# An attention layer's output projection: from four-head accumulation to seven block products

## The chip, the cores and the metric

The kernel runs on one core of one Trainium2 chip. The metric is device time in microseconds (us) of one execution. The engines are named as the profile names them: PE is TensorE's matmuls and PEld its weight loads, DVE is VectorE, ACT is ScalarE, POOL is GpSimd, and SP is SyncE, whose queue issues every DMA of this kernel.

## The reference

One transformer layer on 8 sequences of 512 tokens with 512 features: latent attention with 16 heads, then a gated feed-forward part. Cut to what matters:

```python
x = x + attn(layernorm(x))          # x: (8, 512, 512), float32
x = x + ffn(layernorm(x))

def attn(h):
    q = rmsnorm(h @ wq_a.T) @ wq_b.T           # 16 heads of 128 + 64 (rotary)
    kv_c, k_pe = split(h @ wkv_a.T)            # latent of 128, rotary of 64
    k_nope, v = split(rmsnorm(kv_c) @ wkv_b.T) # 16 heads of 128 and 128
    attn = softmax(q @ k.T * SCALE)            # per batch and head, 512 x 512
    out = (attn @ v).reshape(b, s, 16 * 128)
    return out @ wo.T                          # 2048 -> 512
```

The kernel multiplies the value and output weights of each head into one 128x512 matrix ahead of time ("wvo"), so that a head contributes (attn @ latent) @ wvo to the output. The output projection is then, for each batch, a product of a 512x2048 matrix (16 heads of 128) with a 2048x512 one, added to x.

## The kernel before, in words

`attention` runs over 8 batches x 16 heads x 4 query tiles of 128 tokens: 512 steps (L549). A dictionary `later` holds, per step, the functions to be called at it, and the loop at L613 calls them in order; so the order of issue is written out by hand, though the framework's scheduler may move an instruction among others that don't depend on it, and chooses the buffers and waits.

A step issues the scores of its tile (`scores`, L487): one f32 matmul of 128x512 and two in the single-pass f32r format, into a PSUM tile `sc`, of which there are four (L253). VectorE takes the row maximum (L499), ScalarE the exponential with its sum (L502). One step later VectorE divides (L507) and transposes 32x32 blocks (L156); at every second step the result goes through DRAM and comes back in key-major order as `prT` (`send`, L161: a store and four loads on SyncE's queue). Five steps after a head's last tile `attend` (L512) multiplies by the latent and ScalarE copies the result to `o` (L520), with 128 features on the partitions and 512 tokens along the row. `project` (L452) makes the next head's queries and issues the rotary part, whose sum is made on GpSimd (L360).

After every fourth head, `output` (L526) adds a group of four heads to x: for each of four token tiles, four f32 matmuls of 512 columns accumulate over the heads into a PSUM tile of the pool `ps_mm` (two buffers, L252), and VectorE adds that to `x` (L537). The five functions go to steps 7, 8, 11, 12 and 13 after the last tile of the group's last head (L626). The last of them stores x to DRAM when the fourth group is done (L541). The four `wvo` tiles stay in SBUF for all batches; `fold_o` (L319) makes them during batch 0.

While batch b runs, `prepare` (L579) loads x of batch b+1 and `latents` (L365) makes its normalised, transposed latents, in pieces spread over heads 5 to 12; x is held in two buffers. GpSimd and VectorE also round the feed-forward weights to 8 bits in pieces (`round_piece`, L329) during batches 1 to 6. In the last batch those weights are loaded into the places of weights no longer needed (L600 to L606): the three parts of `wu` where `wvo` lay.

`ffn` (L640) then goes over the 8 batches: matmuls in f32r, two for each product (a high and a low part of the operand).

[...] In `attention` two go to `ps_mm`, four to the scores, one to transposes and one to `attend`.

Of the kernel before, what the change touches and what calls it, by code (L numbers as in the profile page):

```python
# [32 lines left out]
F32 = mybir.dt.float32  # L34
# [7 lines left out]
P = 128  # L42
# [7 lines left out]
G = 4  # L50
# [34 lines left out]
class Layer:  # L85
    def __init__(self, ctx, tc, ins, out):
# [3 lines left out]
        self.xp = ctx.enter_context(tc.tile_pool(name="x", bufs=2))  # L90
        self.dram = dram = ctx.enter_context(tc.tile_pool(name="scratch", bufs=1, space=bass.MemoryType.DRAM))
        self.ident = self.wp.tile([P, P], F32, tag="ident", name="ident")
        make_identity(nc, self.ident)
        self.eps_ln = self.wp.tile([P, 1], F32, tag="eps_ln", name="eps_ln")
# [5 lines left out]
        self.ffn_w = {}  # L100
        self.scratch = {
            (w, i // n): dram.tile([P, n, H], F32R, tag=f"{w}d{i // n}", name=f"{w}d{i // n}")
            for w, n in (("wg", 3), ("wu", 4), ("wd", 4))
            for i in range(0, NI, n)
        }
        self.size = {"wg": 3, "wu": 4, "wd": 4}
# [9 lines left out]
    def load_ffn(self, w, k, pool, tag):  # L116

        n = self.size[w]
        t = pool.tile([P, n, H], F32R, tag=tag, name=f"{w}{k}")
        self.nc.sync.dma_start(t.bitcast(F32), self.scratch[w, k].bitcast(F32))  # L120
        for j in range(n):
            self.ffn_w[w, k * n + j] = t[:, j, :]
# [64 lines left out]
    def ffn_parts(self):  # L187
        return (
            self.xp.tile([P, NC, S], F32R, tag="lat", name="yh"),
# [25 lines left out]
    def ffn_normed_blocks(self, x, small, work):  # L215
# [4 lines left out]
        y = self.wp.tile([P, 2, NQ, NC, 2 * Q], F32, tag="tok", name="y")  # L220
# [5 lines left out]
        def apply(t):  # L226
            xn = work.tile([P, H], F32, tag="xn", name="xn")
# [18 lines left out]
    def attention(self):  # L246
        tc, nc, ins, wp, xp = self.tc, self.nc, self.ins, self.wp, self.xp
        with ExitStack() as ctx:
# [4 lines left out]
            ps_sc = ctx.enter_context(tc.tile_pool(name="ps_sc", bufs=4, space=PSUM))  # L253
            ps_t = ctx.enter_context(tc.tile_pool(name="ps_t", bufs=1, space=PSUM))
            ps_av = ctx.enter_context(tc.tile_pool(name="ps_av", bufs=1, space=PSUM))

            def load_x(src):

                x = xp.tile([P, NT, H], F32, tag="x", name="x")
# [8 lines left out]
            wlr = wp.tile([P, NC, RL], F32, tag="wlr", name="wlr")  # L268
# [5 lines left out]
            xs = {0: x}  # L274
# [4 lines left out]
            wqp_s, wa_s, wvo_s = [], [], []  # L279
# [39 lines left out]
            def fold_o(h):  # L319

                g, j = divmod(h, G)
                wv, wo = fold.pop(("o", h))
                if j == 0:
                    wvo_s.append(wp.tile([P, G, H], F32, tag=f"wvo{g}", name=f"wvo{g}"))
                ps = ps_mm.tile([P, H], F32, tag="mm", name="wvo_ps")
                nc.tensor.matmul(ps, wv, wo, start=True, stop=True)  # L326
                nc.scalar.activation(wvo_s[g][:, j, :], ps, AF.Identity, scale=knw)
# [37 lines left out]
            def latents(b):  # L365


                x = xs[b]
# [400 lines left out]
```

## Time and profile before

| what | us |
|---|---|
| three timed runs | 2802.70, 2803.81, 2803.94 |
| median | 2803.81 |
| the profiled execution | 2803.76 |
| its span, from first to last instruction | 2802.0 |
| TensorE's granted clock in it | 0.997 of full |

Busy time of the engines in stretches of the span that are about a batch of attention each, and in the feed-forward part, in us:

| from | to | PE | DVE | ACT | POOL |
|---|---|---|---|---|---|
| 600 | 875 | 275.0 | 190.4 | 93.2 | 33.0 |
| 1150 | 1425 | 274.7 | 193.1 | 92.5 | 32.4 |
| 1980 | 2270 | 286.1 | 173.8 | 83.3 | 10.5 |
| 2270 | 2800 | 526.5 | 195.0 | 163.5 | 126.8 |

A row says for how long each engine had an instruction running in the stretch. Matmuls overlap their neighbours, so a share near the whole means that one was always in flight, and not that the array was at its best.

All DMAs together move 359.9 MB, at 128 GB/s over the span; their packets keep the 16 DMA engines busy for 41% of it. The largest parts are the stores and loads of the transposed weights of attention: 256 stores of 512 KB (median 2.8 us from issue to landing) and 1024 loads of 128 KB (3.5 us).

### The profile page before, as it was taken

What the parts mean: (1) busy time and instruction counts of PE and PEld (TensorE: products, weight loads), DVE (VectorE), ACT (ScalarE), POOL (GpSimd) and SP (SyncE); (2) the same over time, 40 slices, a digit from 0 to 9 for tenths busy, and PEclk for the clock granted to TensorE, in tenths of its full rate; (3) what the DMA queues carried; (4) which work ended last, traced back from release to release, by engine and by line L of the source; (5) the groups of instructions that cost most, each with busy time, mean ns of one, the idle gap of its engine ahead of it and who ended that gap; (6) DMA issues with size and microseconds to landing.
All of it is one profiled execution on the core that took longest, in us unless ns stands there. A gap on an engine that the chain in (4) does not pass through costs nothing.

```text
span 2802.0 us, 27010 instructions
## 1 busy us (share of the span) xinstructions
PE 2777.7 (99%) x8496; PEld 1566.6 (56%) x8496; DVE 1706.1 (61%) x3584; ACT 916.3 (33%) x1956; POOL 351.4 (13%) x341
## 2 busy tenths in 40 slices
PE   8999999999999999999999999999999999999999
PEld 4555445444544454455444544554444468888887
DVE  5756676776676767676766676666666634433332
ACT  3333333333332333233333332333233233222222
POOL 2000101210020011000200021000000012222222
PEclk9999999999999999999999999999999999999999
DMA  4634454445445534453445344533455541111110
GB/s 141 195 117 139 135 165 129 140 146 158 122 134 153 169 106 143 150 166 111 139 143 165 117 147 137 165 113 120 148 167 162 149 151 60 61 64 64 60 64 19
DMA packets 240047, 359.87 MB, mean 128 GB/s; under 512 B 27168, under 2 KB 190112, under 8 KB 237216
## 3 DMA queue, kind: packets, MB, share of 16 engines
q1 hardware_dynamic: 239904, 358.14, 41.3%
q8 instruction: 68, 1.11, 0.2%
q14 instruction: 75, 0.61, 0.1%
HBM read 190.27 MB, written 167.77 MB: 128 GB/s over the span
## 4 chain that ended last, share of the span: by engine, by line
PE 98%; DVE 1%; ACT 1%; DMA 0%; POOL 0%; issue 0%; SPq 0%; ACTq 0%; POOLq 0%; DVEq 0%
PE wo_ps L534 16%; PE sc L495 16%; PE av L517 15%; PE qn_ps L467 11%; PE sc L497 8%; PE pu L668 6%; PE pg L668 6%; PE pd L694 6%; PE qpe_ps L461 6%; PE lr_ps L393 4%; PE ln_pt L148 1%; PE wvo_ps L326 0%; PE lat_pt L426 0%; PE wa_ps L311 0%; DMA x<-in_hid 0%
## 5 line engine op out<-in xcount | busy, mean ns | idle before, releaser
L502 ACT ACTIVATE pr<-sc,nmax 128x512 f32<-128x512 f32 x512 | 351.6, 687 | 781.3 <-DVE nmax L499 585.2
L497 PE MATMUL sc<-kpe,qpe 128*128 128x512 f32 x1024 | 530.4, 597 | 0.3 <-DVE qpe L479 0.3
L495 PE MATMUL sc<-lat,qn 128*128 128x512 f32 x1024 | 523.3, 592 | 2.0 <-ACT qn L469 1.6
L499 DVE TENSOR_REDUCE nmax<-sc 128x1 f32<-128x512 f32 x512 | 349.5, 684 | 257.1 <-PE sc L497 254.7
L534 PE MATMUL wo_ps<-wvo,o 128*128 128x512 f32 x1024 | 466.0, 595 | 3.5 <-ACT o L520 3.2
L517 PE MATMUL av<-prT,kvt 128*128 128x512 f32 x1024 | 461.2, 592 | 0.0
L156 DVE STREAM_TRANSPOSE block<-pr 128x512 f32<-128x512 f32 x512 | 358.3, 705 | 10.3
L467 PE MATMUL qn_ps<-lat,wa 128*128 128x512 f32 x768 | 352.7, 593 | 0.0
L497 PEld LDWEIGHTS sc<-kpe,qpe 128*128 128x128 f32 x1024 | 194.0, 190 | 246.3 <-issue 235.1
L517 PEld LDWEIGHTS av<-prT,kvt 128*128 128x128 f32 x1024 | 192.3, 190 | 216.1 <-issue 207.0
L534 PEld LDWEIGHTS wo_ps<-wvo,o 128*128 128x128 f32 x1024 | 191.5, 190 | 206.0 <-issue 180.5
L495 PEld LDWEIGHTS sc<-lat,qn 128*128 128x128 f32 x1024 | 191.0, 190 | 162.9 <-issue 139.9
L507 DVE TENSOR_SCALAR pr<-pr,rden 128x512 f32<-128x512 f32 x512 | 273.0, 533 | 13.5
L467 PEld LDWEIGHTS qn_ps<-lat,wa 128*128 128x128 f32 x768 | 145.8, 190 | 161.5 <-issue 150.1
L360 POOL TENSOR_TENSOR roped<-rope_own,rope_sw 128x512 f32<-128x512 f32 x72 | 94.4, 1312 | 1072.7 <-DVE rope_sw L359 899.2
L678 DVE SCALAR_TENSOR_TENSOR fuse<-pu,us,gate 128x512 f32<-128x512 f32 x96 | 71.8, 749 | 203.3 <-PE pu L668 192.2
L682 POOL TENSOR_TENSOR fl<-fuse,fh 128x512 fp32r<-128x512 f32 x96 | 126.8, 1322 | 454.5 <-ACT fh L681 374.7
L506 DVE RECIPROCAL rden<-den 128x1 f32<-128x1 f32 x512 | 77.9, 152 | 164.3 <-ACT pr L502 162.4
L461 PE MATMUL qpe_ps<-lat,wqp 128*128 128x512 f32 x384 | 177.5, 596 | 0.0
L74 POOL TENSOR_TENSOR q_r<-raw,q_m 128x256 f32<-128x256 f32 x72 | 54.0, 750 | 872.9 <-DVE q_m L72 760.6
L668 PE MATMUL pg<-yh,wg 128*128 128x512 f32 x384 | 151.8, 395 | 1.0 <-DVE x L537 0.8
L668 PE MATMUL pu<-yh,wu 128*128 128x512 f32 x384 | 152.4, 397 | 0.0
(93 smaller groups left out, 2884.7 us busy)
## 6 DMA issues: line engine op xcount, KB each, us to landing
way<-block SPq DMA_DIRECT2D x256, 512.0 KB, 2.8
prT<-way SPq DMA_DIRECT2D x1024, 128.0 KB, 3.5
x<-in_hid SPq DMA_DIRECT2D x32, 256.0 KB, 4.6
x<-x SPq DMA_DIRECT2D x8, 1024.0 KB, 4.4
out<-o SPq DMA_DIRECT2D x32, 256.0 KB, 2.0
fx<-x SPq DMA_DIRECT2D x7, 1024.0 KB, 5.1
way<-y_block SPq DMA_DIRECT2D x14, 512.0 KB, 2.6
y<-way SPq DMA_DIRECT2D x56, 128.0 KB, 2.8
```

The lines of the kernel that those rows point to most:

```text
L156: self.nc.vector.transpose(out[:, :, :, i : i + Q].rearrange("p c k i -> p k c i"), x.rearrange("p (k c j) -> p k c j", c=NQ, j=Q),)
L461: nc.tensor.matmul(ps, wqp_s[g][:, r, pj * P : (pj + 1) * P], lat[:, r, :], start=r == 0, stop=r == NR - 1)
L467: nc.tensor.matmul(ps, wa_s[g][:, j, r, :], lat[:, r, :], start=r == 0, stop=r == NR - 1)
L495: nc.tensor.matmul(sc, qn[:, q], lat[:, NR, :], start=True, stop=False)
L497: nc.tensor.matmul(sc, qpe[:, h % 2, q], kpe[:, part, :], start=False, stop=part == 1)
L499: nc.vector.tensor_reduce(nmax, sc, AX.X, ALU.max, negate=True)
L502: nc.scalar.activation(pr, sc, AF.Exp, bias=nmax, accum_out=den)
L507: nc.vector.tensor_scalar(pr, pr, rden, None, ALU.mult)
L517: nc.tensor.matmul(av, kvt[:, kt, :], prT[:, :, :, kt, :], start=kt == 0, stop=kt == NT - 1)
L534: nc.tensor.matmul(ps, o[j][:, t * P : (t + 1) * P], wvo_s[g][:, j, :], start=j == 0, stop=j == G - 1)
L668: nc.tensor.matmul(ps, w[name, i][:, c * P : (c + 1) * P], y[k][:, c, :], start=c == 0 and k == 0, stop=c == NC - 1 and k == 1,)
L694: nc.tensor.matmul(pd, f[:, i, t * P : (t + 1) * P], w["wd", i], start=i == 0 and f is fh, stop=i == NI - 1 and f is fl,)
```

## The change

Strassen's scheme, in Winograd's form with seven products, replaces the eight block products of a 2x2 block multiplication. A group of four heads is two head pairs. For each pair the left matrix has two token halves (256 tokens each) as block rows and the even and odd head as block columns; the right one (`wvo`) has the even and odd head as block rows and two feature halves of 256 as block columns.

- `sums` makes the four sums of the left blocks of a pair, on GpSimd, one step after the pair's second `attend`: S3 = A11 - A21, S1 = A21 + A22 (in the place of A21), S2 = S1 - A11, S4 = A12 - S2.
- `fold_o` writes the three blocks that are used as they are into a tile of seven (`wst`), and GpSimd makes the four sums T1 to T4 in batch 0. The tile is stored to DRAM (`wst_d`), since seven blocks of all groups don't fit in SBUF beside the rest. From batch 1 on, `load_wst` loads each group's tile in four pieces, into two buffers that rotate.
- `output` makes seven products. Each is four matmuls with 256 columns (two token tiles of the half x two head pairs, accumulated). They share PSUM tiles: `u` (a bank of its own, pool `ps_o`) takes A11 B11, then on top of it S2 T2, S3 T3 and A22 T4; `v` takes S1 T1 and then S4 B22; `z` takes A12 B21. After each product VectorE adds the tile as it then stands to a quarter of x, seven additions of 128x512 elements in all. In four of the five functions there are two, one, two and two products.
- The bank for `u` comes from the scores, which have three tiles instead of four.
- x has one buffer in place of two: `prepare` loads x of the next batch into the tile `tok`, in which `latents` also writes its result, and x is loaded once more, at step 3 of head 3 of its own batch, to be added to.
- `wu` is kept in two parts of six instead of three of four; the first is loaded into a `wst` buffer in the last head of attention, the second after attention, and `wd` is loaded whole at the start of the feed-forward part. There, tiles take other places (`y`, `xn`, `o`, and x in turn in two tiles).

```diff
-        self.xp = ctx.enter_context(tc.tile_pool(name="x", bufs=2))
+        self.xp = ctx.enter_context(tc.tile_pool(name="x", bufs=1))
...
+        self.size = {"wg": 3, "wu": 6, "wd": 4}
...
+        self.wst_d = [
+            dram.tile([P, 2, 7, H // 2], F32, tag=f"wst_d{g}", name=f"wst_d{g}") for g in range(NG)
+        ]
...
-            ps_sc = ctx.enter_context(tc.tile_pool(name="ps_sc", bufs=4, space=PSUM))
+            ps_sc = ctx.enter_context(tc.tile_pool(name="ps_sc", bufs=3, space=PSUM))
             ps_t = ctx.enter_context(tc.tile_pool(name="ps_t", bufs=1, space=PSUM))
+            ps_o = ctx.enter_context(tc.tile_pool(name="ps_o", bufs=1, space=PSUM))
...
             def fold_o(h):
...
-                ps = ps_mm.tile([P, H], F32, tag="mm", name="wvo_ps")
-                nc.tensor.matmul(ps, wv, wo, start=True, stop=True)
-                nc.scalar.activation(wvo_s[g][:, j, :], ps, AF.Identity, scale=knw)
+                    wst_s[0, g] = wp.tile([P, 2, 7, H // 2], F32, tag="wst", name="wst", bufs=2)
+                ps = ps_mm.tile([P, 2, H // 2], F32, tag="mm", name="wvo_ps")
+                nc.tensor.matmul(ps.rearrange("p u n -> p (u n)"), wv, wo, start=True, stop=True)
+                w = wst_s[0, g][:, j // 2]
+                place = w[:, 1:3, :] if j % 2 else w[:, 0:7:6, :]
+                nc.scalar.activation(place, ps, AF.Identity, scale=knw)
+                if j % 2:
+                    for out, m, n in ((3, 6, 0), (5, 2, 6), (4, 2, 3), (6, 1, 4)):
+                        nc.gpsimd.tensor_tensor(w[:, out, :], w[:, m, :], w[:, n, :], ALU.subtract)
+                    nc.sync.dma_start(self.wst_d[g][:, j // 2], w)
+
+            def load_wst(b, g):
+                def piece(p, lo, hi):
+                    if (b, g) not in wst_s:
+                        wst_s[b, g] = wp.tile([P, 2, 7, H // 2], F32, tag="wst", name="wst", bufs=2)
+                    nc.sync.dma_start(wst_s[b, g][:, p, lo:hi, :], self.wst_d[g][:, p, lo:hi, :])
+                return [lambda p=p, k=k: piece(p, *k) for p in range(2) for k in ((0, 3), (3, 7))]
...
-                tok = wp.tile([P, NT, RQ + 2 * DR], F32, tag="tok", name=f"tok_{b}")
+                tok = toks.pop(b)
+                x = tok if b else xs[0]
...
+            def sums(b, h):
+                even, odd = (state["o", b, h - 1 + k].rearrange("p (u s) -> p u s", u=2) for k in range(2))
+                s = hp.tile([P, 3, S // 2], F32, tag="sums", name="sums", bufs=3)
+                s2, s3, s4 = (s[:, k, :] for k in range(3))
+                nc.gpsimd.tensor_tensor(s3, even[:, 0], even[:, 1], ALU.subtract)
+                nc.gpsimd.tensor_tensor(even[:, 1], even[:, 1], odd[:, 1], ALU.add)
+                nc.gpsimd.tensor_tensor(s2, even[:, 1], even[:, 0], ALU.subtract)
+                nc.gpsimd.tensor_tensor(s4, odd[:, 0], s2, ALU.subtract)
+                state["sums", b, h] = even[:, 0], even[:, 1], s2, s3, s4, odd[:, 0], odd[:, 1]
+
             def output(b, g):
...
-                def tile(t):
-                    ps = ps_mm.tile([P, H], F32, tag="mm", name="wo_ps")
-                    for j in range(G):
-                        nc.tensor.matmul(
-                            ps, o[j][:, t * P : (t + 1) * P], wvo_s[g][:, j, :], start=j == 0, stop=j == G - 1
-                        )
-                    nc.vector.tensor_tensor(x[:, t, :], x[:, t, :], ps, ALU.add)
+                A11, S1, S2, S3, S4, A12, A22 = range(7)
+                B11, B21, B22, T1, T2, T3, T4 = range(7)
+                got = {}
+
+                def product(name, left, right, c, last=True):
+                    first = name not in got
+                    if first:
+                        pool, tag = (ps_o, "o") if name == "u" else (ps_mm, "mm")
+                        got[name] = pool.tile([P, 2, H // 2], F32, tag=tag, name=f"{name}_ps")
+                    for t in range(2):
+                        for p in range(2):
+                            nc.tensor.matmul(
+                                got[name][:, t, :], ops[p][left][:, t * P : (t + 1) * P], w[:, p, right, :],
+                                start=first and t == 0 and p == 0, stop=last and t == 1 and p == 1, skip_group_check=True,
+                            )
+                    nc.vector.tensor_tensor(c, c, got[name], ALU.add)
...
-                return [lambda t=t: tile(t) for t in range(NT)] + [store]
+                return [
+                    lambda: (product("u", A11, B11, c11, False), product("z", A12, B21, c11)),
+                    lambda: product("u", S2, T2, c12, False),
+                    lambda: (product("u", S3, T3, c22, False), product("v", S1, T1, c22, False)),
+                    lambda: (product("v", S4, B22, c12), product("u", A22, T4, c21)),
+                    store,
+                ]
...
-                xs[b] = load_x(hidden(b))
+                toks[b] = load_x(hidden(b), wp, "tok")
...
+            for b in range(1, B):
+                for g in range(NG):
+                    for k, f in enumerate(load_wst(b, g)):
+                        later[at[b, G * g + 3, 3] - 17 + 2 * k].append(f)
+                later[at[b, 3, 3]].append(lambda b=b: xs.__setitem__(b, load_x(hidden(b))))
...
+                    if h % 2:
+                        later[i + 6].append(lambda b=b, h=h: sums(b, h))
```

## The prediction

> **What bounds the kernel now.** I read four views in this order: the page's busy shares and chain of waits, the listing of instruction groups by shape, a stretch of the timeline for the price of one matmul, and the waits.
>
> ```profile
> span 2802.0 us, 27010 instructions
> PE 2777.7 (99%) x8496; PEld 1566.6 (56%) x8496; DVE 1706.1 (61%) x3584; ACT 916.3 (33%) x1956; POOL 351.4 (13%) x341
> PEclk9999999999999999999999999999999999999999
> PE 98%; DVE 1%; ACT 1%; DMA 0%; POOL 0%; issue 0%; SPq 0%; ACTq 0%; POOLq 0%; DVEq 0%
> PE wo_ps L534 16%; PE sc L495 16%; PE av L517 15%; PE qn_ps L467 11%; PE sc L497 8%; PE pu L668 6%; PE pg L668 6%; PE pd L694 6%; PE qpe_ps L461 6%; PE lr_ps L393 4%; PE ln_pt L148 1%; PE wvo_ps L326 0%; PE lat_pt L426 0%; PE wa_ps L311 0%; DMA x<-in_hid 0%
> ```
>
> The chain is TensorE for 98%, at full clock, and the output projection (L534) is 16% of it. A busy PE is not a PE at its peak, so I checked whether those matmuls follow each other without holes. They do:
>
> ```profile
> 1000.96 3.98 PEld L393 LDWEIGHTS lr_ps<-wlr,xT 128*128 128x128 f32 x16
> 1001.19 4.04 PE L393 MATMUL lr_ps<-wlr,xT 128*128 128x384 f32 x16
> ...
> 1005.07 3.60 PE L517 MATMUL av<-prT,kvt 128*128 128x512 f32 x8
> ...
> 1008.50 1.02 PE L495 MATMUL sc<-lat,qn 128*128 128x512 f32 x2
> ```
>
> One f32 matmul leaves two records, each with its weight load. Eight records of 512 columns fill 1005.07 to 1008.50: 3.43 us, 0.429 us each. The 16 records of L393 (eight of 384 columns, eight of 192) fill 1001.19 to 1005.07: 3.88 us, 0.485 for one of each. With a fixed part a and a slope b: a + 512b = 0.429 and 2a + 576b = 0.485 give b = 0.833 ns per column and a = 2.7 ns. Priced so, and at the 0.23 us spacing that the FFN matmuls show, all matmuls come to about 2760 us of the 2802. Some 10 us lie before the first and after the last; most of the rest is in the serial start (0 to 50 us). Nothing but less TensorE work can help much.
>
> ```profile
> L534 PE MATMUL wo_ps<-wvo,o 128*128 128x512 f32 x1024 | 466.0, 595 | 3.5 <-ACT o L520 3.2 <-ACT qn L469 0.3
> L537 DVE TENSOR_TENSOR x<-x,wo_ps 128x512 f32<-128x512 f32 x128 | 87.1, 681 | 104.4 <-PE wo_ps L534 103.9
> L74 POOL TENSOR_TENSOR q_r<-raw,q_m 128x256 f32<-128x256 f32 x72 | 54.0, 750 | 872.9 <-DVE q_m L72 760.6 <-DMA prT<-way 95.2 <-DVE rden L506 16.9
> DVE x L537 <- PE wo_ps L534: 103.9, 79, 17.0
> L507 DVE TENSOR_SCALAR pr<-pr,rden x512: 442/486/1592, 53.8 to 2244.5; 128x512 f32<-128x512 f32 x171
> ```
>
> The first three give counts, mean durations and idle time; the fourth says that in 79 of 128 cases VectorE stood waiting for the product, so that its add began at once. The last is the spread of one VectorE operation (shortest, median, longest).
>
> **What the Trainium skill says.** "TensorE: Matmul & The Clock Gate", Back-to-back issue gap, gives N/2.4 + 2.5 ns for a warm matmul of N columns; with an f32 record streaming twice its columns that is 429 ns for 512, as measured, and it agrees with the two-point fit. "GPSIMD Engine Reference", Specifications, says that GpSimd shares its SBUF interfaces with VectorE and contends with operations in a two-port mode or with two SBUF inputs. The trace agrees for L507: median 486 ns, mean 533, longest 1592; the long ones lie beside a POOL add. "PSUM — Partial Sum Buffer", The four PSUM rules, allows a synchronised read of a partial sum in the middle of an accumulation group. The change needs that; no run here shows it yet.
>
> **The change part by part.** *Matmuls.* Before: 8 batches x 4 groups x 4 token tiles x 4 heads = 512 matmuls, 1024 records x 0.429 = 439.3 us. After: 7 products x 2 token tiles x 2 head pairs = 28 matmuls of 256 columns for each of 32 groups, 1792 records. A record takes 2.7 + 256 x 0.833 = 215.9 ns, so 386.9 us. The doubt is the weight load: its record lasts 190 ns, and there are more of them. But 192-column records follow each other at 0.162 us with the same load, so it does not bind at 0.216. Gain: 52.4 us, 1.64 per group, all on the path.
>
> *Adds.* Seven VectorE adds of 128x512 per group for four: 96 x 0.681 = +65 us. GpSimd's subtractions contend as well: the mean of L507 over its median costs 512 x 0.047 = 24 us today, against 208 us of POOL time between 50 and 2270 us (the listing of busy time by stretch). New POOL work is 64 head pairs x 4 x 0.75 = 192 us, and 24 us for the weight sums of batch 0, so about 25 us more on VectorE. By the same listing VectorE is busy 1489 us of those 2220 (67%); after, 1579 of 2168 (73%). Beside TensorE, so at nothing on average; what it can cost is in the waits below.
>
> *New waits of TensorE.* u and v are read by VectorE and then accumulated on. Per group there are four such waits: u before S2, u before S3, v before S4, u before A22. All matmuls behind the waiting one stand still, scores too. Naked, one costs an add (0.68) and two handovers (about 0.1 each; in the serial start TensorE resumed 0.68 us after a 0.585 us ScalarE copy), some 0.85 us. By the order in the source, z (1.73 us) and a score step (two f32 records and two single-pass ones, 1.3 us) lie behind the first u, three steps behind the second, a product and scores behind the fourth: covered. Only v has just the scores' 1.3 us, enough if VectorE is free at once. It was in 79 of 128 cases; in the other third I take 0.5 us late: 32 x 0.15 = 5 us. Bounds 0 and 32 x 0.85 = 27.
>
> *Score buffers, 4 to 3.* I set the start of each score matmul in the timeline against the end of the exponential three steps earlier. In 29 of 509 it starts before that end, by 62 us in all: 24 in batches 0 to 6 (mostly head 5, where the next batch's moments fill VectorE) and 38 in the last. That is the upper bound. Other products can be put in the holes, and in the last batch the lag comes from SyncE: its load of wu (L120) waits for wo_ps 21.8 us, the block transposes wait for sends behind it, and that load is moved. The lower bound is 0; I take 6.
>
> *GpSimd's sums.* S2 needs three of the four subtractions, 2.3 us after ScalarE's copy of o. A projection (2.6 to 5.1 us), scores and two products lie before it: hidden. Only behind the last head nothing else lies: its u and z take 3.45 us, then u before S3 and v before S4 are nearly naked. I take 2 us.
>
> *DMA.* 28 x 1.84 MB of sums, 7.3 MB stored, 7 MB of x: 360 to 426 MB. SyncE issues 148 more DMAs at about 0.43 us: 64 us over the whole, beside work. A piece of 0.4 to 0.5 MB delays what is behind it by the 2.8 us that a 0.5 MB send takes at most; the last prT landing stands 1.9 us (least) to 10 us (median) before its matmul. A buffer of sums is free three steps before SyncE asks, the x buffer's store is issued three steps before its reload. Cost 0, bound 10. In batch 0 each store of sums holds SyncE behind ScalarE and four subtractions, some 4 us, eight times: inside the same slack. The FFN's late half of wu (1.5 MB) is wanted six blocks of 16 matmuls (22 us) after the FFN begins; 1 MB took 5.3 us: covered. FFN tiles only change places.
>
> *Sum.* 2802.0 - 52.4 + 5 + 6 + 2 = 2762.6 of span, and 1.8 around it (the profiled execution took 2803.76, the median shown is 2803.81): 2764 us.
>
> **Rivals.** *A: the score buffers cost most of their bound.* 24 us in batches 0 to 6, a third of the 38 in the last: 2749.6 + 37 + 5 + 2 + 1.8 = 2795 us. For it: the counted overlaps. Against: they assume an order of matmuls that nothing fills.
> *B: slower.* The shared accumulators pace TensorE. If the products are issued closer together than the source has them, u and v alternate with VectorE's adds. It decides at 1.64 us per group, two naked waits of four; with three, 3 x 0.85 x 32 = 82 us: 2749.6 + 82 + 1.8 = 2833 us. For it: wo_ps matmuls of two tiles are seen interleaved before their scores, so the order isn't that of the source, and VectorE reaches 73%. Against: three waits have 3 us of other work before them.
> *C: nothing new is late,* and the last batch's holes go too: 2749.6 - 2 + 1.8 = 2749 us. For it: TensorE idles only some 10 us between 50 us and the end today.
> *D: it doesn't do what it says*, if narrow records cost as much as wide ones: 28/16 of 439 us, 330 us slower. The 192-column records exclude it.
>
> **How the numbers follow.** My forecast 0.62, C 0.10, A 0.17, B 0.11. What can be told from no change here is about 0.2%, 5.6 us. A still ends 9 us below before; its upper tail gives the 0.02 for no change. Faster 0.87, slower 0.11. The range: the upper end is A's, which leaves B and A's tail outside; the lower is C's with 3 us for the fit.
>
> **What would show it.** The L534 group replaced by 1792 records of 128x256, spaced 0.216 us; at 0.24 or more the first step is wrong. "PE waits for DVE x" in the waits at under 10 us: right; tens: B. Scores (L495) waiting for ACT pr above 20 us: A. av waiting for DMA prT at all: the DMA step is wrong. L507's mean should rise from 533 to about 580 ns.

## The result, and the profile after

| what | before | after |
|---|---|---|
| median of the timed runs, us | 2803.26 | 2921.89 |
| lowest and highest, us | 2799.90, 2803.94 | 2921.27, 2922.89 |
| span of the profiled execution, us | 2802.0 | 2919.3 |
| the profiled execution itself, us | 2803.76 | 2921.27 |
| TensorE's granted clock in it | 0.997 | 0.990 |

The kernel before was timed again beside the changed one, hence 2803.26. The ratio after to before is 1.0426, with a 95% interval of 1.0408 to 1.0444: the change costs 118.6 us. The forecast was a gain of 40.

From the page of the changed kernel: its shares, TensorE's row of slices, its chain, two of its groups and the DMA issues.

```profile
span 2919.3 us, 29079 instructions
PE 2776.6 (95%) x9264; PEld 1709.7 (59%) x9264; DVE 1761.3 (60%) x3680; ACT 912.8 (31%) x1968; POOL 565.9 (19%) x629
...
PE   8999999998999899989998999899988889999999
...
PE 29%; DVE 2%; ACT 1%; POOL 1%; issue 1%; DMA 0%; SPq 0%; ACTq 0%; POOLq 0%; DVEq 0%
...
L522 PE MATMUL sc<-lat,qn 128*128 128x512 f32 x1024 | 535.0, 604 | 42.1 <-ACT pr L529 42.0
L529 ACT ACTIVATE pr<-sc,nmax 128x512 f32<-128x512 f32 x512 | 350.3, 686 | 571.6 <-DVE block L163 354.5
...
way<-block SPq DMA_DIRECT2D x256, 512.0 KB, 3.0
prT<-way SPq DMA_DIRECT2D x1024, 128.0 KB, 3.4
...
wst<-wst_d SPq DMA_DIRECT2D x56, 512.0 KB, 4.9
```

And from the kernel before, its row of slices and the same two groups in the listing by shape:

```profile
PE   8999999999999999999999999999999999999999
L495 PE MATMUL sc<-lat,qn 128*128 128x512 f32 x1024 | 523.3, 592 | 2.0 <-ACT qn L469 1.6 <-ACT pr L502 0.4
L502 ACT ACTIVATE pr<-sc,nmax 128x512 f32<-128x512 f32 x512 | 351.6, 687 | 781.3 <-DVE nmax L499 585.2 <-DVE block L156 112.3 <-DVE rden L506 81.9
```

TensorE's share fell from 99% to 95%, and its row of slices, all nines after the first before, now dips at a steady distance: once per batch of attention (a batch is some 290 us, a slice 73), and throughout the last batch. The chain of waits could be followed for only a third of the span here. The scores (L522) wait 42.0 us for the exponentials, against 0.4 before (L495), and the exponentials wait 354.5 us for the block transposes of VectorE (L163), against 112.3. Yet the sends (`way`, `prT`) land as quickly as before: medians of 3.0 and 3.4 us against 2.8 and 3.5.

The groups of the output projection, in the listing by shape (columns: busy time, mean ns of one; idle time before them, and what ended it):

```profile
L588 PE MATMUL u_ps<-wst,o 128*128 128x256 f32 x512 | 133.0, 397 | 11.4 <-ACT o L547 11.1 <-DVE x L592 0.3
L588 PE MATMUL u_ps<-wst,sums 128*128 128x256 f32 x512 | 131.0, 389 | 11.7 <-DVE x L592 9.7
L588 PE MATMUL z_ps<-wst,o 128*128 128x256 f32 x256 | 68.0, 390 | 7.4 <-ACT o L547 7.4
L588 PE MATMUL v_ps<-wst,o 128*128 128x256 f32 x256 | 66.0, 384 | 7.9 <-ACT qn L496 7.8 <-POOL o L561 0.2
L588 PE MATMUL v_ps<-wst,sums 128*128 128x256 f32 x256 | 60.7, 379 | 0.0
```

They are the 1792 records of 256 columns that were forecast, the next one starting after 0.216 us in the median, and the change's own new wait, for VectorE's additions into x (L592), comes to 10.0 us of TensorE's idle time. Counting every matmul of both timelines at the spacing of its shape gives 2759.6 us of work before and 2707.0 after. So 52.6 us of work were saved. What grew is everything else: span less work went from 42 to 212 us. Holes between matmuls, added up from the timeline, went from 19.8 to 138.2 us of that. The clock, asked in short windows, stood at half rate in the middle of the run for 47.8 us in place of 3.4, which is about 22 us of matmul work more. That leaves some 30 us, most of them an effect of the count: a record of 512 columns lasts 592 ns in the profile while the next one can start after 429, so each hole is counted some 0.16 us short, and there are 168 holes in place of 24, which makes an estimate of 23 us. The question of the study was what makes TensorE stand still for so long.

One stretch at head 5 of a batch shows the pattern; the timeline's columns are the start, the length, engine, line and operation:

```profile
975.63 0.49 DVE L534 TENSOR_SCALAR pr<-pr,rden 128x512 f32<-128x512 f32 x1
...
976.17 0.69 DVE L526 TENSOR_REDUCE nmax<-sc 128x1 f32<-128x512 f32 x1
...
976.96 0.49 DVE L534 TENSOR_SCALAR pr<-pr,rden 128x512 f32<-128x512 f32 x1
...
987.70 0.69 DVE L141 BATCH_NORM_STATS2 ln_st<-x 128x6 f32<-128x512 f32 x1
...
990.76 0.48 DVE L408 TENSOR_SCALAR xc<-x,ln_mv 128x512 f32<-128x512 f32 x1
...
991.30 0.66 PE L155 MATMUL ln_pt<-ident,xc 128*128 128x128 f32 x4 [3.07 <-DVE xc L408]
...
992.63 1.27 DVE L163 STREAM_TRANSPOSE block<-pr 128x512 f32<-128x512 f32 x2
...
992.75 0.30 ACT L145 ACTIVATE ln_sd<-ln_mv,eps_ln 128x4 f32<-128x4 f32 x1 [5.04 <-DVE ln_mv L142]
992.96 0.57 ACT L547 COPY o<-av 128x512 f32<-128x512 f32 x1
...
993.58 2.93 PE L588 MATMUL u_ps<-wst,o 128*128 128x256 f32 x6 [1.62 <-ACT o L547]
...
994.84 0.69 ACT L529 ACTIVATE pr<-sc,nmax 128x512 f32<-128x512 f32 x1
```

Two tiles of `pr` are divided at 975.63 and 976.96. The two block transposes that free them come at 992.63, behind the next batch's moments and centring (L141, L408), though VectorE waited for others in between. The row maximum at 976.17 is done at 976.86, but its exponential starts at 994.84, 18 us later, for it needs a free `pr`. Meanwhile TensorE stands still twice, and neither time for an exponential: 3.07 us before L155, the transposes of the next batch's centred tile (xc), and 1.62 us before L588, for the copy of `o`. That copy stands on ScalarE behind the next batch's standard deviation (L145), which itself waits 5.04 us for VectorE. So on all three engines work of the next batch stands ahead of work that is wanted sooner. What follows is in the windows (columns: length; busy time and count of PE, PEld, DVE, ACT and POOL; granted clock, DMA share, GB/s):

```profile
995.00:999.00 4.00, 4.00 (x9) 2.49 (x8) 1.28 (x4) 1.76 (x5) 0.00 (x0) 0.50 0.73 236
999.00:1006.00 7.00, 5.96 (x23) 3.71 (x22) 2.99 (x5) 0.67 (x2) 0.00 (x0) 0.95 0.00 1
```

The clock is at 0.50 after these holes, so TensorE looks fully busy at half its rate.

### The profile page after: what moved, and what is told of

Read it like the earlier page. It is cut to its first block, busy times and chain, and to the rows that moved or that the text cites. A ratio compares the mean times of both kernels' runs of the same rounds, so it can differ in the third digit from the quotient of the medians.

```text
span 2919.3 us, 29079 instructions
## 1 busy us (share of the span) xinstructions
PE 2776.6 (95%) x9264; PEld 1709.7 (59%) x9264; DVE 1761.3 (60%) x3680; ACT 912.8 (31%) x1968; POOL 565.9 (19%) x629
## 5 line engine op out<-in xcount | busy, mean ns | idle before, releaser
L522 PE MATMUL sc<-lat,qn 128*128 128x512 f32 x1024 | 535.0, 604 | 42.1 <-ACT pr L529 42.0
L529 ACT ACTIVATE pr<-sc,nmax 128x512 f32<-128x512 f32 x512 | 350.3, 686 | 571.6 <-DVE block L163 354.5
L524 PE MATMUL sc<-kpe,qpe 128*128 128x512 f32 x1024 | 525.6, 594 | 2.2 <-DVE qpe L506 2.2
L544 PE MATMUL av<-prT,kvt 128*128 128x512 f32 x1024 | 461.0, 592 | 0.0
L163 DVE STREAM_TRANSPOSE block<-pr 128x512 f32<-128x512 f32 x512 | 349.2, 697 | 3.3
L524 PEld LDWEIGHTS sc<-kpe,qpe 128*128 128x128 f32 x1024 | 195.4, 191 | 245.5 <-issue 229.8
L544 PEld LDWEIGHTS av<-prT,kvt 128*128 128x128 f32 x1024 | 192.8, 190 | 214.8 <-issue 203.3
L534 DVE TENSOR_SCALAR pr<-pr,rden 128x512 f32<-128x512 f32 x512 | 283.5, 554 | 12.8
L522 PEld LDWEIGHTS sc<-lat,qn 128*128 128x128 f32 x1024 | 190.2, 193 | 152.9 <-ACT pr L529 70.8
L547 ACT COPY o<-av 128x512 f32<-128x512 f32 x128 | 74.5, 582 | 451.9 <-PE av L544 451.9
L742 PE MATMUL pu<-yl,wu 128*128 128x512 f32 x384 | 150.6, 392 | 0.0
L742 PE MATMUL pg<-yl,wg 128*128 128x512 f32 x384 | 149.4, 389 | 0.0
```

The lines of the kernel that those rows point to most:

```text
L163: self.nc.vector.transpose(out[:, :, :, i : i + Q].rearrange("p c k i -> p k c i"), x.rearrange("p (k c j) -> p k c j", c=NQ, j=Q),)
L522: nc.tensor.matmul(sc, qn[:, q], lat[:, NR, :], start=True, stop=False)
L524: nc.tensor.matmul(sc, qpe[:, h % 2, q], kpe[:, part, :], start=False, stop=part == 1)
L529: nc.scalar.activation(pr, sc, AF.Exp, bias=nmax, accum_out=den)
L534: nc.vector.tensor_scalar(pr, pr, rden, None, ALU.mult)
L544: nc.tensor.matmul(av, kvt[:, kt, :], prT[:, :, :, kt, :], start=kt == 0, stop=kt == NT - 1)
```

## The experiments

Two families of theories stood against each other. *The change's own body*: the score buffers (rival A), the shared accumulators (rival B), GpSimd's sums. *Its surroundings*: the loads of weight tiles and the second load of x, 140 DMA instructions added to SyncE's queue, which the forecast had put at nothing. All ratios are against the kernel before, run on the same chip, with 95% intervals in brackets.

### The score buffer alone

```diff
-            ps_sc = ctx.enter_context(tc.tile_pool(name="ps_sc", bufs=4, space=PSUM))
+            ps_sc = ctx.enter_context(tc.tile_pool(name="ps_sc", bufs=3, space=PSUM))
```

This is an edit of the kernel before.

> The kernel before with three score tiles instead of four, nothing else. Theory S (the score bank given to u starves TensorE): 2803 + 50 to 110, so 2850 to 2915 us, with scores waiting for ACT pr by tens of us. Theory U (TensorE waits for VectorE's adds on the shared tiles u and v) and theory G (the sums on GpSimd and what waits for them): about 2805 to 2815 us.

Measured: 2809.21 us, ratio 1.0022 [1.0011, 1.0033], so +6 us. Its listing of groups:

```profile
L495 PE MATMUL sc<-lat,qn 128*128 128x512 f32 x1024 | 525.4, 595 | 6.4 <-ACT pr L502 4.7
```

The scores' wait for the exponentials rises from 0.4 to 4.7 us. The whole costs the 6 us that the forecast took, and not 42. Rival A is not the cause.

### Each product in its own tile, and the bank given back

```diff
-                    first = name not in got
-                    if first:
-                        pool, tag = (ps_o, "o") if name == "u" else (ps_mm, "mm")
-                        got[name] = pool.tile([P, 2, H // 2], F32, tag=tag, name=f"{name}_ps")
+                    got[name] = ps_mm.tile([P, 2, H // 2], F32, tag="mm", name=f"{name}_ps")
...
-                                start=first and t == 0 and p == 0, stop=last and t == 1 and p == 1, skip_group_check=True,
+                                start=t == 0 and p == 0, stop=t == 1 and p == 1, skip_group_check=True,
```

> The changed kernel, but each product starts a PSUM tile of its own in the two buffers of ps_mm, so no product accumulates on a tile that VectorE still has to read; the seven adds stay as they are. The sums over products that u and v would have carried are left out. Three score tiles, the bank of u unused. Theory U: 2770 to 2810 us. Theory S: within 25 us of 2922. Theory G: within 25 us of 2922.

The second run also drops the pool `ps_o` and gives the scores four tiles again.

> As the run with fresh tiles, but the bank of u goes back to the scores (four tiles). The sums over products are left out. Theory S: 2770 to 2820 us, at least 60 us below its sister with three. Theory U: the two differ by under 15 us.

Measured: 2884.41 us, 1.0296 [1.0266, 1.0325], and 2892.50 us, 1.0324 [1.0295, 1.0354]. Without shared accumulators 81 us of the loss remain, and the fourth score tile brings nothing back. The edit doesn't free the products of VectorE's additions altogether: all seven now take turns in the two buffers of `ps_mm`, and TensorE still waits 15.6 us for the additions in the first of these runs, against 10.1 in the changed kernel. So the 37 us that this run gains can't be read as the price of shared accumulators; the order of all the other work moves with such an edit too.

### Without GpSimd's sums

```diff
-                s = hp.tile([P, 3, S // 2], F32, tag="sums", name="sums", bufs=3)
-                s2, s3, s4 = (s[:, k, :] for k in range(3))
-                nc.gpsimd.tensor_tensor(s3, even[:, 0], even[:, 1], ALU.subtract)
-                nc.gpsimd.tensor_tensor(even[:, 1], even[:, 1], odd[:, 1], ALU.add)
-                nc.gpsimd.tensor_tensor(s2, even[:, 1], even[:, 0], ALU.subtract)
-                nc.gpsimd.tensor_tensor(s4, odd[:, 0], s2, ALU.subtract)
-                state["sums", b, h] = even[:, 0], even[:, 1], s2, s3, s4, odd[:, 0], odd[:, 1]
+                state["sums", b, h] = even[:, 0], even[:, 1], odd[:, 0], even[:, 1], odd[:, 1], odd[:, 0], odd[:, 1]
```

> The changed kernel without the four GpSimd operations per head pair: the products take the plain token halves of o in the places of S1 to S4, so the sums of the left blocks are left out. Theory G: 2790 to 2830 us. Theories S and U: 2890 to 2922 us, since only about 25 us of VectorE's contention with GpSimd goes.

Measured: 2912.93 us, 1.0397 [1.0367, 1.0428]. Leaving out the four sums of the left blocks gives 9 us, and the intervals of the two ratios overlap; they are not the cause. (The sums of the weights, in batch 0, stay.)

### The old products in the new surroundings

```diff
+                def tile(t):
+                    ps = ps_mm.tile([P, 2, H // 2], F32, tag="mm", name="wo_ps")
+                    for j in range(G):
+                        nc.tensor.matmul(
+                            ps.rearrange("p u n -> p (u n)"), left[j][:, t * P : (t + 1) * P],
+                            w[:, j // 2, 1:3, :].rearrange("p u n -> p (u n)"), start=j == 0, stop=j == G - 1,
+                        )
...
-                    lambda: (product("u", A11, B11, c11, False), product("z", A12, B21, c11)),
-                    lambda: product("u", S2, T2, c12, False),
-                    lambda: (product("u", S3, T3, c22, False), product("v", S1, T1, c22, False)),
-                    lambda: (product("v", S4, B22, c12), product("u", A22, T4, c21)),
+                return [lambda t=t: tile(t) for t in range(NT)] + [
```

GpSimd's sums are gone here as well; the loads, the buffers of x and the score tiles are the changed kernel's.

> The changed kernel with the old form of the projection put back inside it: four token tiles of four matmuls of 512 columns and four adds, on the streamed tiles (two plain blocks of each serve as right operand, so the result isn't the projection's); no sums on GpSimd. The streams of weights, the second load of x, three score tiles and the moved tiles of the feed-forward part stay. Theory E (the surroundings cost the time: DMA streams, x through tok): 2880 to 2930 us. Theory P (the seven products themselves, with their finer waits and three more adds): 2805 to 2825 us, as the kernel before with three score tiles.

Measured: 2879.94 us, 1.0276 [1.0246, 1.0306]. Its matmuls are those of the kernel before, 2760 us of work; against that kernel with three score tiles (2809.21) it is 71 us slower. So a loss of this size comes without any of Strassen's products: it is in the surroundings.

### The loads left out, all and each alone

```diff
+                    if (b, g) not in wst_s and (b, g) > (1, 1):
+                        wst_s[b, g] = wst_s[1, g % 2]
...
-                    nc.sync.dma_start(wst_s[b, g][:, p, lo:hi, :], self.wst_d[g][:, p, lo:hi, :])
+                    if b == 1 and g < 2:
+                        nc.sync.dma_start(wst_s[b, g][:, p, lo:hi, :], self.wst_d[g][:, p, lo:hi, :])
...
-                later[at[b, 3, 3]].append(lambda b=b: xs.__setitem__(b, load_x(hidden(b))))
+                later[at[b, 3, 3]].append(lambda b=b: xs.__setitem__(b, xs[0]))
```

The first two parts leave out the weight tiles (those of the first two groups of batch 1 are still loaded, and used for all later ones), the last the second load of x; the three runs make both, the first alone and the last alone.

> The changed kernel with its 51 MB of weight tiles loaded for two groups once and used for all later ones, and x not loaded a second time (the sums run on in the x of batch 0), so right operands and residual are left out of batches 1 to 7. Theory E: 2770 to 2820 us. Theory P: 2895 to 2922 us.

> The changed kernel with the weight tiles of two groups loaded once and used for all later ones (right operands of batches 1 to 7 left out), while x is still loaded twice. If the 51 MB of weight tiles are what costs: 2810 to 2840 us. If it is the second load of x, beside that into tok two steps earlier: 2890 to 2920 us.

> The changed kernel with x loaded only once, into tok (the sums run on in the x of batch 0, so the residual of batches 1 to 7 is left out), while the weight tiles are still streamed. If the weight tiles cost: 2890 to 2920 us. If the second load of x does: 2810 to 2840 us.

| left out | us | ratio |
|---|---|---|
| both | 2810.65 | 1.0029 [1.0015, 1.0042] |
| the weight tiles | 2830.33 | 1.0094 [1.0065, 1.0124] |
| the second x | 2878.61 | 1.0267 [1.0237, 1.0296] |

Without the loads 111 us are gone: 92 go with the weight tiles alone, 43 with x alone, which is more than 111 together, so they aren't two prices that add up. And even without them some 47 us are missing to the forecast of 2764. The waits of the kernel without both (columns: waiting line and what it waited for; us in total, times, longest):

```profile
ACT pr L532 <- DVE block L163: 294.4, 84, 10.1
...
PE sc L525 <- ACT pr L532: 6.4, 8, 2.4
```

The scores' wait is back at 6.4 us, though the exponentials still wait 294.4 us for the transposes, not far from the 354.5 of the changed kernel. The lines L163 and L525 to L532 here are L163 and L522 to L529 of the changed kernel.

### Bytes, or instructions in the queue

Now the loads are back at the same steps, in the same number, each of 16 columns only (but for the two tiles that were loaded there too).

```diff
+            def again(b):
+                xs[b] = xs[0]
+                for t in range(NT):
+                    nc.sync.dma_start(xs[b][:, t, :16], hidden(b)[:, t, :16])
...
+                    else:
+                        nc.sync.dma_start(wst_s[b, g][:, p, lo:hi, :16], self.wst_d[g][:, p, lo:hi, :16])
```

> The run without streams, with the streams' instructions back on SyncE's queue at the same steps, but each moves 16 columns in place of 256 or 512 (right operands and residual of batches 1 to 7 are left out, as there). If what costs is that SyncE has 140 more instructions to issue and to wait for: 2880 to 2922 us. If it is the size of what stands in SyncE's queue (in the planned order or on the chip): 2800 to 2835 us.

And the complete kernel, every byte moved, with these loads issued by GpSimd, or by ScalarE, in place of SyncE:

```diff
-                    nc.sync.dma_start(wst_s[b, g][:, p, lo:hi, :], self.wst_d[g][:, p, lo:hi, :])
+                    nc.gpsimd.dma_start(wst_s[b, g][:, p, lo:hi, :], self.wst_d[g][:, p, lo:hi, :])
...
-                later[at[b, 3, 3]].append(lambda b=b: xs.__setitem__(b, load_x(hidden(b))))
+                later[at[b, 3, 3]].append(lambda b=b: xs.__setitem__(b, load_x(hidden(b), queue=nc.gpsimd)))
```

> The changed kernel, complete, with the loads of weight tiles and the second load of x issued from GpSimd's queue in place of SyncE's: the same bytes at the same steps. Theory Q (the place in SyncE's queue, ahead of the sends of the transposed weights and in the order planned around it): 2800 to 2850 us. Theory D (the bytes themselves, that is the DMA engines shared with the sends): 2905 to 2930 us.

> The same from ScalarE's queue. Theory Q: 2810 to 2870 us, somewhat worse than from GpSimd's since ScalarE issues in order between exponentials. Theory D: 2905 to 2930 us.

| loads | us | ratio |
|---|---|---|
| 16 columns, SyncE | 2901.39 | 1.0355 [1.0334, 1.0375] |
| whole, GpSimd | 2788.58 | 0.9943 [0.9923, 0.9962] |
| whole, ScalarE | 2792.89 | 0.9963 [0.9943, 0.9983] |

This pair settles the first half of the question. Almost no bytes in SyncE's queue cost 91 us over no loads at all; with all bytes from another queue the loss is gone, and the kernel gets some 15 us faster than before. It is even 22 us faster than without the loads, which can't be a price of the loads; something else differs between these kernels. The page of the run with GpSimd's queue:

```profile
span 2788.9 us, 29276 instructions
PE 2731.7 (98%) x9264; PEld 1708.5 (61%) x9264; DVE 1778.7 (64%) x3680; ACT 927.3 (33%) x1968; POOL 650.4 (23%) x769
...
L522 PE MATMUL sc<-lat,qn 128*128 128x512 f32 x1024 | 524.9, 594 | 5.7 <-ACT pr L529 5.7
...
way<-block SPq DMA_DIRECT2D x256, 512.0 KB, 2.9
prT<-way SPq DMA_DIRECT2D x1024, 128.0 KB, 3.7
...
wst<-wst_d POOLq DMA_DIRECT2D x56, 512.0 KB, 8.6
```

The weight tiles land later here (8.6 us against 4.9) and the sends no sooner (3.7 against 3.4 for `prT`), so it isn't that the transfers stood in each other's way. "DMA: Bandwidth & Descriptors" of the Trainium skill, Rules for kernel authors, says that spreading DMAs over the issuing engines brings no bandwidth and only saves issue time. The landing times agree with the first part; the 133 us gained are more than twice the issue time, 140 instructions at some 0.43 us.

### Is SyncE late, or VectorE's order?

A plain reading is left: SyncE, held by the new instructions, issues the sends late, so the transposes' target (`block`, two buffers) is freed late. The timelines speak against it. For each transpose I took when the multiplication before it had ended, how many instructions stood between the two on VectorE, and when the send that empties its buffer had ended; and for each exponential the time since its row maximum (means, us):

| kernel | its time | transpose after its input | instructions between | exponential after row maximum |
|---|---|---|---|---|
| before | 2803 | 0.97 | 1.39 | 0.96 |
| after | 2922 | 4.62 | 5.43 | 5.60 |
| 16 columns, SyncE | 2901 | 4.20 | 4.12 | 4.67 |
| whole, GpSimd | 2789 | 2.46 | 3.15 | 1.73 |
| no loads | 2811 | 3.18 | 3.95 | 2.50 |

In the changed kernel the send that freed the buffer had left the chip on average 12.3 us before the transpose began, and in all of 254 cases at least 1.7 us before it. The sends themselves were issued 0.30 us after the transposes (0.08 before): SyncE was not late. The transposes had their input and their buffer and were not next in VectorE's own order. "TensorE: Matmul & The Clock Gate" of the Trainium skill, Architectural detail, in the paragraph on queue depths, calls VectorE's queue strictly first in, first out; that agrees with the transpose at 992.63 above, which starts behind the moments although its input is 16 us old.

The means don't tell what the lateness costs. Without the loads transposes start 3.18 us late, with about as many instructions between as in the 16-column kernel, which takes 91 us more. So the cost must depend on which work is late, and where.

That order is planned by the framework when the program is built, and the traces show that the plan moves. I numbered equal instructions in turn and counted how many keep their order from one trace to the other (the longest common sequence):

| kernels compared | VectorE | TensorE |
|---|---|---|
| before, with four and with three score tiles | 3528 of 3584 | 8426 of 8496 |
| loads on GpSimd's queue and on ScalarE's | 3616 of 3680 | 9240 of 9264 |
| loads on SyncE's queue (the changed kernel) and on GpSimd's | 2538 of 3680 | 7695 of 9264 |

None of these edits touches an instruction of VectorE or TensorE; the last changes only which engine issues the loads. So the last theory was: the instructions in SyncE's queue change the plan, and the plan is what costs. First a third block buffer, then the order bound by hand.

```diff
-                    block = hp.tile([P, NQ, NT, 2 * Q], F32, tag="block", name="block")
+                    block = hp.tile([P, NQ, NT, 2 * Q], F32, tag="block", name="block", bufs=3)
```

> The changed kernel with three buffers of block in place of two, so that VectorE's transposes need not wait for the store two blocks back. If the chain of late transposes, exponentials and scores (ACT pr waiting for DVE block 354 us, scores for ACT pr) carries much of the loss: 2860 to 2895 us. If it only passes on lateness that comes from elsewhere: 2910 to 2930 us.

> The complete kernel with the streams on GpSimd's queue and three buffers of block. If late transposes still cost TensorE something: 2765 to 2783 us. If the queue was the whole of it: 2784 to 2795 us.

The second also has the loads on GpSimd's queue. For the order, the changed kernel is kept complete, its loads on SyncE, and one constraint is put on the plan: what the source gives to VectorE after a block transpose may not be planned ahead of it.

```diff
+            def after_pin():
+                return tc.issue_after(pin[-1]) if pin else ExitStack()
+
+            def pinned(f):
+                return lambda: pin.append(ins_of(f()))
...
-                later[i + 1].insert(0, scores(b, h, t, block))
+                with after_pin():
+                    f = scores(b, h, t, block)
+                later[i + 1].insert(0, pinned(f))
...
-                    f()
+                    with after_pin():
+                        f()
```

> The changed kernel, complete, its streams on SyncE's queue as they were; only the order is bound: an instruction that the source gives to an engine after a block transpose may not be planned ahead of it on VectorE. Two buffers of block, and nothing else is touched. If the loss is the planned order, in which transposes stand behind later work: 2770 to 2830 us, with the transposes starting on average under 2 us after the multiplication before them (4.6 in the changed kernel, 1.0 before). If SyncE's queue holds the sends up on the chip itself: 2890 to 2930 us.

> The best complete kernel so far (streams on GpSimd's queue, three buffers of block, 2783.85) with the same order bound. If late transposes are still part of what is left above the forecast: 2760 to 2778 us. Otherwise within 6 us of 2784.

| kernel | us | ratio |
|---|---|---|
| third block buffer, loads on SyncE | 2892.22 | 1.032 [1.029, 1.035] |
| order bound, loads on SyncE | 2838.03 | 1.0127 [1.011, 1.0144] |
| third block buffer, loads on GpSimd | 2783.85 | 0.9936 [0.9921, 0.9951] |
| all three together | 2792.93 | 0.9963 [0.995, 0.9976] |

The waits of the run with the order bound (L528 to L537 are L524 to L533 of the changed kernel):

```profile
ACT pr L533 <- DVE nmax L530: 296.2, 149, 4.8
...
ACT pr L533 <- DVE rden L537: 269.5, 172, 5.2
...
PE sc L526 <- ACT pr L533: 27.6, 26, 3.3
...
PE ln_pt L159 <- DVE xc L412: 11.1, 8, 5.0
```

The last of these is, in the changed kernel:

```profile
PE ln_pt L155 <- DVE xc L408: 21.2, 7, 4.9
```

Not an instruction was taken out and no DMA changed its queue, and 84 of the 118.6 us are gone. The exponentials' wait for the transposes, 354.5 us, is not in the list any more; a transpose starts 0.81 us after its input with 0.78 instructions between. SyncE doesn't explain this gain: 1803 of its 1813 DMAs keep their order, and the sends are issued 0.47 us after the transposes, in place of 0.30. But the constraint on VectorE moves the plan of the others too: only 7578 of TensorE's 9264 matmuls keep their order, and 1668 of ScalarE's 1968 instructions. And little of the gain comes by the exponentials: TensorE's wait for them falls from 42.0 to 27.6 us, by 14, its waits for `xc` and `o` by 23 together; the clock stands at half rate for 44.4 us, nearly as before the constraint (47.8). The plan is shown to cost these 84 us, not the lateness of the transposes by itself. By the recorded expectation of 2770 to 2830 us it fell 8 us short, far from the 2890 or more of the rival. What it doesn't give back, some 50 us against the loads on GpSimd's queue, lies in waits such as that for `rden` (269.5 us in place of 82.3): the constraint holds one kind of instruction in its place, and the plan of the others is still another one.

On GpSimd's queue the third buffer brings the transposes near their input without the constraint, as the waits show:

```profile
ACT pr L529 <- DVE nmax L526: 557.3, 279, 7.2
...
ACT pr L529 <- DVE block L163: 62.9, 30, 4.7
...
PE sc L522 <- ACT pr L529: 4.6, 6, 1.0
```

Transposes start 0.91 us after their input there. It has the lowest median of all, 0.9936 of the kernel before or about 18 us less; its lead of 5 us over the one with two block buffers is smaller than the intervals of the two ratios, which overlap. With the constraint on top (the last row) transposes start 0.37 us after their input, sooner than in any other of these kernels, and yet it takes 9 us more: neither the 2760 to 2778 us that late transposes would have left to gain, nor within 6 us of 2784. Sooner transposes are no gain in themselves.

A last step in this direction, putting the stores of the sums in batch 0 and the first load of x on GpSimd's queue as well, went the wrong way.

```diff
-                    nc.sync.dma_start(self.wst_d[g][:, j // 2], w)
+                    nc.gpsimd.dma_start(self.wst_d[g][:, j // 2], w)
...
-                toks[b] = load_x(hidden(b), wp, "tok")
+                toks[b] = load_x(hidden(b), wp, "tok", queue=nc.gpsimd)
```

> As the last, with the stores of the weight sums in batch 0 and the load of x into tok on GpSimd's queue too. Batch 0, still 9 us above its arithmetic, should come down: 2755 to 2775 us. If batch 0 is held by something else: within 5 us of the last run.

Measured: 2794.66 us, 0.9973 [0.9961, 0.9984], 11 us slower than without, outside both of its expectations, though transposes start 0.44 us after their input. An emptier queue of SyncE is not better for that alone.

## Why the prediction was wrong

**The step that failed** is the one on DMA: "SyncE issues 148 more DMAs at about 0.43 us: 64 us over the whole, beside work", with "Cost 0, bound 10". In its place the runs measured 111 us (loads left out) to 133 us (loads on GpSimd's queue). Most facts in that step were right: the sends don't land later, SyncE isn't held, no matmul waits for a weight tile. One was not, and it is small: the late half of `wu`, said to be covered, holds TensorE up for 3.2 us.

```profile
PE pu L742 <- DMA wu<-wud: 3.2, 1, 3.2
```

What the step left out is that the order of the instructions on VectorE, ScalarE and TensorE is itself made by the framework's scheduler, and that new instructions in one queue can change it for the others. The front part of this document says that the scheduler may move an instruction among others that don't depend on it, and the forecast assumed that it would go on as before.

How it then costs, as far as the timelines show: block transposes stand behind some four more instructions on VectorE, so `pr` comes free later, exponentials start 5.60 us after their row maximum in place of 0.96, and scores wait 42 us. Beside that, at head 5 the next batch's centring and copy of `o` come late for TensorE's own order, and it stands still for several microseconds. That the plan is the cause, and not a mere companion, is shown for 84 us by the run that binds part of it. Which part of the plan carries them is not shown: the kernel without the loads has late transposes and takes 2811 us, and the one with the soonest transposes is not the fastest (2792.93 us). It also stays open why the scheduler's plan moves so far when SyncE's queue gets these instructions, and what makes up the other 50 us. A run with all engines' orders bound was not tried. And since leaving something out moves the plan as well, no difference above is the price of the thing left out alone.

**Matmuls:** right. 52.6 us by the count against 52.4, and the records follow each other at the forecast 0.216 us.

**Score buffers:** right, +6.0 measured alone against 6. Rival A was to be read from "scores waiting for ACT pr above 20 us". That sign came up, at 42 us, and pointed to the wrong cause: the wait is the place where late exponentials are felt, and the buffer count did not make them late.

**New waits of TensorE:** right in size. VectorE's additions cost 10 us of idle time in the changed kernel and 2.6 with the loads on GpSimd's queue, against 5. The place was wrong: the forecast had v uncovered, but in the listing all of it stands before u. Rival B's total, 2833 us, happened to be nearer than the forecast's, by luck: its naked waits were to cost 82 us, and the waits for the additions come to 10.

**GpSimd's sums and VectorE's load:** right in direction. L534 takes 554 ns on average, not 580, after 533; and leaving the sums out gives some 9 us, with intervals that overlap, where 2 us of waits were forecast.

**The sign for the DMA step** was "av waiting for DMA prT at all". It didn't come: the group of av (L544) shows no idle time, and the step was wrong all the same. I had watched for a late transfer only.

**The sum, with the failed step mended:** with the loads on another queue the kernel takes 2788.6 us, and 2783.9 with a third block buffer, against a forecast of 2764. Of the 52.6 us a third, some 18, reaches the end. The 20 us missing in the latter are no single wait in the list above: the holes between matmuls still sum to 48 us there in place of 19.8, and I have not taken them apart.

## What to carry to other kernels

When a change adds DMA instructions to a queue that also carries sends on which the inner loop turns, compare the planned order of every engine, not only landing times: for the critical instruction, set its start against the end of its last input and the freeing of its buffer, and count what stands between. If it had both and still started late, look at what stood ahead of it on its engine. What that costs is another question: read it from what ends TensorE's holes, since here a kernel with late transposes was fast. The cheapest test is to issue the new bulk loads from an engine that is otherwise idle; here it was worth 133 us.

## What the runs showed of the hardware

Small holes in TensorE's work cost more than their length. In the changed kernel the clock is at 0.50 for 3.4 or 6.8 us at a time in eight places, 47.8 us in all, against a single one of 3.4 us before. Five of the eight stand at head 5 of five batches in a row, at two holes of 3.1 and 1.6 us, as in the windows at 995 above. "TensorE: Matmul & The Clock Gate" of the Trainium skill, Part 1, describes such a gate: half rate after an idle window of about 3.4 us, full rate after a busy one. The lengths of the slow stretches, once or twice 3.4 us, agree with it. The holes don't: shorter ones are enough, and here the measurement decides. The one slow stretch in the middle of the kernel before comes after a hole of 1.87 us (a line of the timeline and a window, columns as above):

```profile
2217.34 3.32 PE L534 MATMUL wo_ps<-wvo,o 128*128 128x512 f32 x4 [1.87 <-ACT o L520]
...
2217.80:2221.20 3.40, 3.40 (x5) 1.30 (x4) 1.19 (x2) 0.00 (x0) 0.00 (x0) 0.51 0.08 30
```

Nor is every such hole followed by one: of five holes of 2.3 us at the same place of five batches in the 16-column kernel, two were. A late order can thus be paid for twice, in the hole and in the slow matmuls behind it.
